# Narrow-head attention values computed once and spread through DRAM, with other settings for the kernel's planner

## The chip, the core and the metric

The kernel runs on one core of a Trainium2 chip. A core has a matrix engine (TensorE, PE in the profile, with its weight loads as PEld), a vector engine (VectorE, DVE), a scalar engine (ScalarE, ACT), a general engine (GpSimd, POOL) and a queue engine (SyncE, SP) that here only issues DMA transfers. Each engine works through its own list of instructions in order and waits on semaphores for the others. Data lie in DRAM (HBM), in the on-chip SBUF and in eight banks of PSUM, where PE writes.

The metric is the device time of one execution in microseconds (us). Three executions and one profiled execution are shown for the kernel before.

## What is computed

Sixteen sequences of 128 tokens by 128 features (`x`) pass through four layers; each layer adds a gated cross-attention to a context of 16 x 77 x 96 (`ctx_768`), and then a gated feed-forward part. All is in fp32.

```python
x = x + tanh(g_xattn[0]) * narrow_attention(layernorm(x), ctx_768)   # 16 heads of 8
x = x + tanh(g_ffn[0])   * top2_of_8_experts(layernorm(x))           # 128 -> 512 -> 128, gelu
x = x + tanh(g_xattn[1]) * wide_attention(layernorm(x), ctx_768)     # 16 heads of 64
x = x + tanh(g_ffn[1])   * weighted_linear_experts(layernorm(x))
x = x + tanh(g_xattn[2]) * one_head_attention(layernorm(x), ctx_768)
x = x + tanh(g_ffn[2])   * top1_of_8_experts(layernorm(x))           # silu
x = x + tanh(g_xattn[3]) * narrow_attention(layernorm(x), ctx_768)   # as in layer 0
x = x + tanh(g_ffn[3])   * ternary_ffn(layernorm(x))
```

The narrow attention, which the change touches:

```python
q = (x @ wq + bq).reshape(B, Sq, 16, 8)
k = (y @ wk + bk).reshape(B, Sk, 16, 8)
v = (y @ wv + bv).reshape(B, Sk, 16, 8)
attn = softmax(einsum('bqhd,bkhd->bhqk', q, k) / sqrt(8))
out = einsum('bhqk,bkhd->bqhd', attn, v).reshape(B, Sq, 128) @ wo + bo
```

## The kernel before

**Groups.** The batch of 16 is worked on in four groups (NG = 4) of four sequences (GB = 4). In names such as `a0_2` or `f2_1`, a is attention and f is feed-forward, the first number the layer, the second the group (for `f0` and `f2`, whose experts take two groups together, the half of the batch).

**Narrow heads** (`narrow_heads`, from L828). The sixteen heads are handled four at a time: the keys of four heads lie side by side, masked so that each head meets only its own eight features, which gives 4 x 77 = 308 key positions (PK). With three chunks of 103 (CH) the attention weights are turned and multiplied with the values. So for each sequence the values must be had in a layout in which the 77 context rows stand four times one after the other, as three chunks of 103 rows by 128 features (309 rows, one of them a pad). `narrow_values` (from L806) makes it by brute force: the host has laid the context four times along its columns (`ctx4`); for each sequence SP loads the 309 columns, PE multiplies them with the value weights in three matmuls of 103 rows, ACT or DVE copies the 103 x 384 result from PSUM (`evac`, L622, which may go to either engine), and POOL multiplies it with the head mask `mine`. A matmul in fp32 is two instructions in the profile, so these are 192 instructions for 32 sequences (layers 0 and 3, 16 each).

**Experts.** In layers 0 and 2, `route_half` ranks the tokens of one half, `send` computes the place of each token by a matmul (`place_ps`), and POOL scatters the rows to DRAM (`sorted_x`) by indirect DMA. `sorted_experts` (L1382) loads the sorted rows (`rows_..`), turns them on PE (`rT_ps`), loads each expert's weights (`wx_..`, 578 KB each) and computes hidden layer (`h_ps`) and output (`y_ps`); outputs go to DRAM (`sorted_y`) through SP and are fetched back by indirect DMA (`take_back`). All these transfers but the indirect ones stand in SP's queue.

**Wide heads.** Layer 1 multiplies the value and output weights of each head into one matrix first (`fused`, L925: `heads1`, `heads2`), sends the values that follow to DRAM (`all_u`, by `send_values`) and loads them back in another layout, in pieces of 256 KB and 52 KB.

**The planner.** The program is first recorded as operations with their dependencies (class `Program`), and only then ordered. Every recorded call is emitted from one place, so nearly all profile lines are L535; a normalisation shows as L710 when it went to ACT and L712 when it went to DVE, and weight loads whose expert is read at run time show as L1411 and L1412. `forward` (L305) is a list scheduler: again and again it places the ready operation that is estimated to start first, with a bias against operations late in the order of the pass (`bias`) and a weight on VectorE's duration (`busy`). SBUF is 680 pages of 64 floats for each partition and PSUM eight banks; a tile takes neighbouring pages from its first to its last user, and the operation that takes pages must wait for the former users. Three settings say who may take them: `reserve` (L353, set at L605) is how many pages must stay free when an operation takes new ones while older tiles have none yet; `ahead` is how far past the oldest operation not yet placed an operation may be and still take new pages; `lead` is how long before its latest useful time a DMA may be placed. `arrange` (L456) runs six rounds of a forward and a backward pass, each giving the order of the next, and keeps the best; `emit` writes the operations out. On the chip nothing of the estimates remains but the order on each engine, the choice between engines and the places of the tiles.

Of the kernel before, what the change touches and what calls it, by code (L numbers as in the profile page):

```python
# [11 lines left out]
F32 = mybir.dt.float32  # L12
# [7 lines left out]
B, S, D = 16, 128, 128  # L20
SK, DC = 77, 96
KP = 112
GB = 4
# [4 lines left out]
PK = 4 * SK  # L28
CH = 103
# [186 lines left out]
class Program:  # L216
# [88 lines left out]
    def forward(self, order, ahead, bias, busy, lead):  # L305
# [21 lines left out]
        ready = set()  # L327
# [35 lines left out]
        while len(out) < len(ops):  # L363
            best = None
            for keep in (True, False):
                for n in ready:
                    op = ops[n]
                    got = None
                    for e, when, us in zip(op.engines, op.when, op.us):
                        t = max(free[e], when)  # L370
                        if e == "tensor" and op.first_mode != mode:
                            t = max(t, free[e] + self.TURN)
                        if e in op.port:
                            t = max(t, port)
                        if op.size:
                            t = max(t, op.latest - lead)
                        if op.table not in (None, table):
                            t += self.LOAD
                        cost = us * weigh[e] + bias * (op.pos - oldest)
                        if best is not None and (t + cost if keep else op.pos) > best[0][0]:  # L380
                            continue
                        if got is None:
                            got = place(op, keep, t)
                        if got is None:
                            break
                        if op.pos > oldest + ahead and got[1] and keep:
                            if not any(x.left == 1 and x.slot >= 0 for x in op.tiles):
                                break
                        t = max(t, got[0])
                        key = (t + cost, op.pos) if keep else (op.pos, t)  # L390
                        if best is None or key < best[0]:
                            best = (key, op, e, t, got[1], us)
                if best is not None:
                    break
            if best is None:
                return None
            _, op, e, t, got, us = best
            op.engine, op.start = e, t
            op.end = clock.run(t, us, op.dense) if e == "tensor" else t + us
            free[e] = op.end  # L400
            if e in op.port:
                port = op.end
            if op.table is not None:
                table = op.table
            if e == "tensor":
                mode = op.mode
            if op.after:
                wire = max(wire, op.end) + op.size / self.RATE
                op.end = wire + op.after
            for tl, i in got:  # L410
                tl.slot = i
                spaces[tl.room].take(i, tl.pages)
                unplaced[tl.room].remove(tl.nth)
            ready.discard(op.n)
            out.append(op.n)
            for m in self.back[op.n]:
                ops[m].left -= 1
                if not ops[m].left:
                    get_ready(ops[m])
            for tl in op.tiles:  # L420
                tl.left -= 1
                if not tl.left:
                    when = max(u.end + self.LAG[u.engine] for u in tl.users)
                    spaces[tl.room].give(tl.slot, tl.pages, when)
            while oldest < len(ops) and ops[order[oldest]].end is not None:
                oldest += 1
# [26 lines left out]
            op.latest = length - ends[n]  # L453
        return sorted(range(len(ops)), key=lambda n: (-ends[n], n))

    def arrange(self, rounds=6, ahead=400, bias=0.002, busy=0.3, lead=10.0):  # L456

        ops = self.ops
        self.back = [[] for _ in ops]
        for op in ops:  # L460
            for d in op.deps:
                self.back[d].append(op.n)
        order, best = sorted(range(len(ops)), key=lambda n: ops[n].order), None
        for _ in range(rounds):
            length = self.forward(order, ahead, bias, busy, lead)
            if length is None:
                break
            if best is None or length < best[0]:
                places = {t: t.slot for op in ops for t in op.tiles}
                best = length, [(op.start, op.end, op.engine) for op in ops], places  # L470
            order = self.backward()
        assert best is not None, "no room for any tile"
        self.length, times, places = best
        for op, (op.start, op.end, op.engine) in zip(ops, times):
            pass
        for t, t.slot in places.items():
            pass
        return sorted(ops, key=lambda op: (op.start, op.n))
# [107 lines left out]

@with_exitstack
def tile_gated_blocks(
    ctx: ExitStack, tc: tile.TileContext, x, ctxa, ctx4, cols, rows, b2s, emb, wqo0, wkv0, wx0,
    wq1, wk1, wv1, wo1, we1, wq2, wkv2, wx2, wqo3, wkv3, wf3, out,  # L590
):
    whole = ctx.enter_context(tc.tile_pool(name="whole", bufs=1))
    psum = ctx.enter_context(tc.tile_pool(name="psum", bufs=1, space=PSUM))

    slots = {
        "mv": 4, "st": 6, "ve": 4, "rstd": 4, "mx": 6, "rs1": 5, "rs2": 4, "off": 4,
    }
    low = "middle at v3 ys back junk wT g_gt8 g_eq8 g_lt8"
    shared = {
        "sc": ("psum", True), "bank": ("psum", False),  # L600
        **{tag: ("sbuf", False) for tag in low.split()},
        **{tag: ("sbuf", True) for tag in ("large", "kk", "heads1", "heads2", "we1_sb")},
    }
    pages = {"sbuf": 680, "psum": 8}
    nc = Program(tc.nc, tc, slots, pages, shared, {"sbuf": 20, "psum": 2})  # L605

    class Tiles:
        def tile(self, shape, dtype=F32, tag=None, name=None):
# [2 lines left out]
    sb = Tiles()  # L611
# [7 lines left out]
    def mm_tile(name):  # L619
        return sb.tile([P, 512], F32, tag="bank", name=name)  # L620

    def evac(o, i):  # L622
        nc.either.copy_any(o, i)
# [17 lines left out]
    def col(name, i=0, n=None):  # L641
        at, w = COLS[name]
        return cs[:, at + i : at + (w if n is None else i + n)]
# [16 lines left out]
    for i, layer in enumerate((0, 1, 3)):  # L660
        o = bos[:, i * D : (i + 1) * D]
# [141 lines left out]

    def narrow_values(g, wv, n):  # L806
        got = []
        for b in range(GB):
            at = (g * GB + b) * PK
            cx = sb.tile([KP, 3 * CH], F32, tag="v3", name=f"cx_{n}_{b}")  # L810
            nc.sync.dma_start(cx, ctx4[:, at : at + 3 * CH])
            vp = mm_tile(f"v_ps_{n}_{b}")[:, : 3 * D]
            with nc.together():
                for c in range(3):
                    nc.tensor.matmul(
                        vp[:CH, c * D : (c + 1) * D],
                        lhsT=cx[: DC + 1, c * CH : (c + 1) * CH], rhs=wv,
                        start=True, stop=True,
                    )
            vr = sb.tile([CH, 3, 4, 32], F32, tag="v3", name=f"vr_{n}_{b}")  # L820
            evac(vr, vp[:CH].rearrange("p (c k d) -> p c k d", c=3, k=4))
            vb = sb.tile([CH, 3, 4, 32], F32, tag="v3", name=f"vb_{n}_{b}")
            mask = mine[:CH].rearrange("p c h d -> p c (h d)")[:, :, None, :].to_broadcast([CH, 3, 4, 32])
            nc.gpsimd.tensor_tensor(vb, vr, mask, ALU.mult)
            got.append(vb)
        return got

    def narrow_heads(layer, wqo, wkv, bq, row, t, groups):  # L828
        for g in groups:
            n = f"a{layer}_{g}"  # L830
# [10 lines left out]
                col("hmask")[:, None, :, None].to_broadcast(shape),  # L841
                ALU.mult,
            )
            vbs = narrow_values(g, wkv[: DC + 1, D : 2 * D], n)
            xnT = transposed(layernorm(g, n), n)
            add_row(g, row)
            q = q_proj(xnT, wqo[:, :D], bq, n)
# [759 lines left out]
    def gate(i):  # L1607
        return tg[:, i : i + 1]
# [3 lines left out]
    for t in sorted_x:  # L1612
        k = t.shape[0] // P
        nc.gpsimd.dma_start(
            t.rearrange("(k p) d -> p k d", p=P), zero[:, None, :].to_broadcast([P, k, D])
        )
    a0 = (0, wqo0_sb, wkv0_sb, col("bq0"), 0, gate(0))
    narrow_heads(*a0, [0])

# [62 lines left out]
def _arrays(i):  # L1682
# [3 lines left out]
    def padded(a):  # L1686
        return np.concatenate([a, np.zeros((KP - DC - 1, a.shape[1]), np.float32)], axis=0)
# [6 lines left out]
    def by_head(w):  # L1694
# [25 lines left out]
    }  # L1720
    ctxT = i["ctx_768"].reshape(B * SK, DC).T
    ctxa = np.concatenate([ctxT, np.ones((1, B * SK), np.float32)], axis=0)
    ctx4 = np.broadcast_to(ctxa.reshape(DC + 1, B, 1, SK), (DC + 1, B, 4, SK)).reshape(DC + 1, -1)
    return {
        "x": i["x"],
        "ctxa": padded(ctxa),
        "ctx4": padded(np.concatenate([ctx4, ctx4[:, : 3 * CH - PK]], axis=1)),
        "cols": np.concatenate([parts[n] for n, _ in _WIDTHS], axis=1),
        "rows": _wide(np.concatenate([i["L0_xattn_bo"], i["L1_xattn_bo"], i["L3_xattn_bo"]])),
        "b2s": i["L1_ffn_expert_b"],  # L1730
# [40 lines left out]
```

## Time and profile before

Three executions took 760.32, 767.32 and 770.58 us.

| | us |
|---|---|
| median of three executions | 767.32 |
| the profiled execution, whole | 769.02 |
| its span in the trace | 767.2 |
| mean granted clock of TensorE | 0.911 of full speed |

The profile is that of one execution. Its busy times are of each engine alone; they overlap, and an engine that is busy need not be what the end waits for. The order of the program shows in the stages, whose busy times in us are:

| stage of the trace, us | what is mainly worked on | length | PE | DVE | ACT | POOL | clock |
|---|---|---|---|---|---|---|---|
| 0-115 | narrow heads of layer 0, first half's routing | 115 | 93.35 | 92.33 | 60.25 | 49.68 | 0.93 |
| 115-153 | end of those heads, fused weights | 38 | 31.19 | 13.18 | 13.65 | 11.76 | 0.76 |
| 153-268 | layer 0's experts, layer 1's values | 115 | 97.40 | 41.47 | 57.46 | 30.72 | 0.90 |
| 268-450 | layers 1 and 2 for three groups | 182 | 173.73 | 146.68 | 106.39 | 91.12 | 0.99 |
| 450-479 | last wide heads, loads for layer 2's experts | 29 | 20.90 | 20.01 | 12.33 | 12.43 | 0.92 |
| 479-529 | layer 2's experts, first half | 50 | 49.98 | 27.19 | 31.48 | 11.04 | 0.98 |
| 529-575 | last one-head attention, second half's routing | 46 | 28.10 | 36.73 | 16.02 | 26.63 | 0.65 |
| 575-640 | second half's experts, start of layer 3 | 65 | 60.20 | 38.16 | 40.28 | 13.13 | 0.93 |
| 640-767 | layer 3 | 127.2 | 105.39 | 86.44 | 74.36 | 28.15 | 0.89 |

The clock is what the chip granted to TensorE in that stage. Where the profile names "another core or an unknown queue", the release could not be traced to one of the engines.

### The profile page before, as it was taken

What the parts mean: (1) busy time and instruction counts of PE and PEld (TensorE: products, weight loads), DVE (VectorE), ACT (ScalarE), POOL (GpSimd) and SP (SyncE); (2) the same over time, 40 slices, a digit from 0 to 9 for tenths busy, and PEclk for the clock granted to TensorE, in tenths of its full rate; (3) what the DMA queues carried; (4) which work ended last, traced back from release to release, by engine and by line L of the source; (5) the groups of instructions that cost most, each with busy time, mean ns of one, the idle gap of its engine ahead of it and who ended that gap; (6) DMA issues with size and microseconds to landing.
All of it is one profiled execution on the core that took longest, in us unless ns stands there. A gap on an engine that the chain in (4) does not pass through costs nothing.

```text
span 767.2 us, 15064 instructions
## 1 busy us (share of the span) xinstructions
PE 660.2 (86%) x5408; PEld 528.9 (69%) x5408; DVE 502.2 (65%) x1322; ACT 412.2 (54%) x898; POOL 274.7 (36%) x311
## 2 busy tenths in 40 slices
PE   4889886996698999999998996999557999688996
PEld 3578764776697989567657744988334898565785
DVE  5877993374121478588787886547697833687764
ACT  2756632564254678554555553565325576377853
POOL 4630456025203154485353354106735103521010
PEclk9999985998698999999999998999558999979898
DMA  4100911495448885323324149821105422000000
GB/s 127 44 9 19 310 41 62 157 346 191 130 142 258 272 249 161 106 72 111 85 70 130 36 124 329 280 63 51 35 0 166 153 59 67 15 1 2 1 29 29
DMA packets 86394, 86.87 MB, mean 113 GB/s; under 512 B 6144, under 2 KB 75744, under 8 KB 86320
## 3 DMA queue, kind: packets, MB, share of 16 engines
q1 hardware_dynamic: 80368, 75.55, 31.6%
q0 software_dynamic: 3840, 9.31, 3.6%
q10 hardware_dynamic: 2112, 1.05, 0.5%
q8 instruction: 43, 0.70, 0.4%
q14 instruction: 31, 0.25, 0.1%
HBM read 63.61 MB, written 22.28 MB: 112 GB/s over the span
## 4 chain that ended last, share of the span: by engine, by line
PE 66%; DVE 17%; issue 4%; DMA 4%; ACT 4%; another core or an unknown queue 2%; SPq 2%; POOL 1%; POOLq 0%; DVEq 0%; ACTq 0%
PE banks L535 66%; DVE shared L535 4%; ACT shared L535 3%; DVE mx_a L535 2%; DVE shared L712 2%; SPq L535 2%; DVE x L535 1%; DMA shared<-all_u 1%; DMA shared<-sorted_x 1%; DVE rs_a L535 1%; ACT shared L710 1%; DMA x<-in_x 1%; DVE st_f L535 1%; DMA sorted_y<-shared 1%
## 5 line engine op out<-in xcount | busy, mean ns | idle before, releaser
L535 PE MATMUL banks<-shared 128*128 128x128 f32 (+7 forms) x3040 | 368.8, 325 | 37.2 <-issue 15.7
L535 PEld LDWEIGHTS banks<-shared 128*128 128x128 f32 (+4 forms) x3040 | 294.9, 180 | 93.0 <-issue 45.8
L535 ACT COPY shared<-banks 128x512 f32<-128x512 f32 (+10 forms) x261 | 149.7, 600 | 132.3 <-PE banks L535 116.2
L535 PE MATMUL banks<-ident,shared 128*128 128x128 f32 (+3 forms) x829 | 132.8, 305 | 40.2 <-DVE shared L712 11.5
L535 PEld LDWEIGHTS banks<-ident,shared 128*128 128x128 f32 (+3 forms) x829 | 107.6, 165 | 74.2 <-issue 24.3
L535 ACT ACTIVATE shared<-banks,shared 128x128 f32<-128x128 f32 x304 | 85.6, 378 | 65.8 <-PE banks L535 25.6
L535 ACT ACTIVATE shared<-shared 128x616 f32<-128x616 f32 (+1 forms) x100 | 70.2, 707 | 61.4 <-DVE shared L535 50.1
L535 DVE TENSOR_REDUCE mx_a<-banks 128x8 f32<-128x616 f32 (+1 forms) x100 | 77.2, 773 | 14.4 <-PE banks L535 8.8
L535 DVE TENSOR_TENSOR shared<-banks,shared 128x128 f32<-128x128 f32 (+1 forms) x84 | 26.9, 327 | 88.5 <-PE banks L535 42.9
L535 DVE TENSOR_TENSOR shared<-banks,mx_a 128x616 f32<-128x616 f32 (+1 forms) x100 | 78.1, 781 | 6.3 <-remote 2.0
L535 POOL DMA_INDIRECT shared<-sorted_y,idx_f x48 | 46.7, 973 | 70.1 <-DMA shared<-in_wx 36.7
L535 POOL DMA_INDIRECT sorted_x<-shared,idx_f x48 | 47.4, 988 | 48.1 <-DVE r_both_f L535 23.6
L535 DVE COPY shared<-banks 103x512 f32<-103x512 f32 (+8 forms) x47 | 30.6, 655 | 48.5 <-PE banks L535 44.0
L535 POOL TENSOR_TENSOR shared<-shared,mine 103x384 f32<-103x384 f32 x32 | 32.8, 1038 | 79.0 <-ACT shared L535 54.8
L535 POOL TENSOR_TENSOR shared<-shared,rs_a 128x616 f32<-128x616 f32 x32 | 38.6, 1218 | 52.5 <-DVE rs_a L535 34.6
L535 POOL TENSOR_TENSOR rstd_f<-ve_f,nhalf 128x4 f32<-128x4 f32 x16 | 16.4, 1022 | 83.4 <-DVE ve_f L535 69.4
L535 PE MATMUL banks<-shared,ctx_sb 96*128 96x512 f32 (+1 forms) x80 | 37.9, 598 | 1.7 <-DVE shared L535 1.0
L535 POOL TENSOR_TENSOR x<-x,shared 128x128 f32<-128x128 f32 x64 | 28.7, 456 | 25.2 <-ACT shared L535 13.6
L535 PE MATMUL banks<-ctx_sb,shared 96*128 96x308 f32 x128 | 37.2, 426 | 0.0
L535 POOL TENSOR_TENSOR rstd_a<-ve_a,nhalf 128x4 f32<-128x4 f32 x16 | 16.6, 1038 | 48.4 <-DVE ve_a L535 44.3
L535 ACT ACTIVATE shared<-banks,cols_sb 128x128 f32<-128x128 f32 (+1 forms) x44 | 21.1, 520 | 22.1 <-PE banks L535 18.6
L535 PEld LDWEIGHTS banks<-wkv_sb,shared 97*103 97x103 f32 x192 | 25.8, 191 | 7.5 <-DVE shared L535 3.6
(207 smaller groups left out, 711.3 us busy)
## 6 DMA issues: line engine op xcount, KB each, us to landing
shared<-in_wx SPq DMA_DIRECT2D x60, 578.0 KB
shared<-all_u SPq DMA_DIRECT2D x32, 256.0 KB
sorted_y<-shared SPq DMA_DIRECT2D x76, 64.0 KB
shared<-in_ctx SPq DMA_DIRECT2D x32, 135.2 KB
all_u<-shared SPq DMA_DIRECT2D x14, 308.0 KB
shared<-sorted_x SPq DMA_DIRECT2D x6, 512.0 KB
sorted_x<-shared POOLq DMA_DIRECT2D x2, 1472.0 KB
shared<-sorted_x SPq DMA_DIRECT2D x4, 448.0 KB
```

The costliest lines, as they stand in the source:

```text
L535: getattr(engine, f)(*(_real(a) for a in args), **done)
L710: engine.activation(o.made(), i.made(), AF.Identity, bias=k.made(), scale=r.made())
L712: engine.tensor_scalar(o.made(), i.made(), m.made(), r.made(), ALU.subtract, ALU.mult)
```

## The change

Two things are changed together.

First, `send_narrow_values` computes the values of a group once: four matmuls with the 97 x 77 context as weights (the 97th row holds the ones that carry the bias), one 77 x 512 copy from PSUM, and for each sequence a store by SP that writes the 77 x 128 values four times one below the other into a new DRAM tensor `all_v` (154 KB, in pieces of 512 bytes). `narrow_values` then loads the 309 x 128 rows of each sequence back as three chunks of 103 rows, also through SP and 154 KB, and masks them on POOL as before. The pad row of `all_v` is set to zero by a DMA of POOL at the start. The input `ctx4` is dropped. Over the eight groups this is 32 matmuls in place of 96, eight copies in place of 32, and 64 transfers in place of 32.

Second, the planner's settings: `ahead` from 400 to 800, `bias` from 0.002 to 0.0022, `busy` from 0.3 to 0.07, `lead` from 10.0 to 10.8, the reserve from 20 pages and 2 banks to 0 pages and 1 bank, and ready operations are tried in the order of their numbers.

```diff
-                for n in ready:
+                for n in sorted(ready):
...
-    def arrange(self, rounds=6, ahead=400, bias=0.002, busy=0.3, lead=10.0):
+    def arrange(self, rounds=6, ahead=800, bias=0.0022, busy=0.07, lead=10.8):
...
-    nc = Program(tc.nc, tc, slots, pages, shared, {"sbuf": 20, "psum": 2})
+    nc = Program(tc.nc, tc, slots, pages, shared, {"sbuf": 0, "psum": 1})
...
-    def narrow_values(g, wv, n):
+
+    shape_v = [B, 3 * CH, D]
+    all_v = nc.tile(shape_v, F32, "dram", "all_v", real=tc.dram_tile(shape_v, F32, name="all_v"))
+
+    def send_narrow_values(g, wv, n):
+
+        mm = mm_tile(f"v_ps_{n}").rearrange("p (b d) -> p b d", b=GB)
+        with nc.together():
+            for b in range(GB):
+                nc.tensor.matmul(
+                    mm[:SK, b, :], lhsT=ctx_of(g, b), rhs=wv, start=True, stop=True
+                )
+        v = sb.tile([SK, GB, D], F32, tag="middle", name=f"v_{n}")
+        evac(v, mm[:SK])
+        for b in range(GB):
+            nc.sync.dma_start(
+                all_v[g * GB + b : g * GB + b + 1, :PK].rearrange("o (h k) d -> (o k) h d", h=4),
+                v[:, b, None, :].to_broadcast([SK, 4, D]),
+            )
+
+    def narrow_values(g, n):
         got = []
         for b in range(GB):
-            at = (g * GB + b) * PK
-            cx = sb.tile([KP, 3 * CH], F32, tag="v3", name=f"cx_{n}_{b}")
-            nc.sync.dma_start(cx, ctx4[:, at : at + 3 * CH])
-            vp = mm_tile(f"v_ps_{n}_{b}")[:, : 3 * D]
-            with nc.together():
-                for c in range(3):
-                    nc.tensor.matmul(
-                        vp[:CH, c * D : (c + 1) * D],
-                        lhsT=cx[: DC + 1, c * CH : (c + 1) * CH], rhs=wv,
-                        start=True, stop=True,
-                    )
             vr = sb.tile([CH, 3, 4, 32], F32, tag="v3", name=f"vr_{n}_{b}")
-            evac(vr, vp[:CH].rearrange("p (c k d) -> p c k d", c=3, k=4))
+            nc.sync.dma_start(
+                vr.rearrange("p c k d -> p c (k d)"),
+                all_v[g * GB + b : g * GB + b + 1].rearrange("o (c p) d -> (o p) c d", c=3),
+            )
             vb = sb.tile([CH, 3, 4, 32], F32, tag="v3", name=f"vb_{n}_{b}")
...
-            vbs = narrow_values(g, wkv[: DC + 1, D : 2 * D], n)
+            send_narrow_values(g, wkv[: DC + 1, D : 2 * D], n)
+            vbs = narrow_values(g, n)
...
+    nc.gpsimd.dma_start(all_v[:, PK:].rearrange("b r d -> (b r) d"), zero[:B])
```

With other settings and other operations the planner gives another order on every engine, and another placing of the tiles.

More of the change, by code (lines that the diff above doesn't have):

```diff
@@ L588, in tile_gated_blocks @@
 def tile_gated_blocks(
-    ctx: ExitStack, tc: tile.TileContext, x, ctxa, ctx4, cols, rows, b2s, emb, wqo0, wkv0, wx0,
+    ctx: ExitStack, tc: tile.TileContext, x, ctxa, cols, rows, b2s, emb, wqo0, wkv0, wx0,
     wq1, wk1, wv1, wo1, we1, wq2, wkv2, wx2, wqo3, wkv3, wf3, out,
@@ L1722, in _arrays @@
     ctxa = np.concatenate([ctxT, np.ones((1, B * SK), np.float32)], axis=0)
-    ctx4 = np.broadcast_to(ctxa.reshape(DC + 1, B, 1, SK), (DC + 1, B, 4, SK)).reshape(DC + 1, -1)
     return {
@@ L1726, in _arrays @@
         "ctxa": padded(ctxa),
-        "ctx4": padded(np.concatenate([ctx4, ctx4[:, : 3 * CH - PK]], axis=1)),
         "cols": np.concatenate([parts[n] for n, _ in _WIDTHS], axis=1),
```

## The prediction

> **What bounds the kernel now.** I read the page's busy times, slices and chain shares first, then the groups kept apart by shape, then busy time by stage, then the chain of waits in three windows, and last what the SyncE queue (SPq) waited for.
>
> ```profile
> PE 660.2 (86%) x5408; PEld 528.9 (69%) x5408; DVE 502.2 (65%) x1322; ACT 412.2 (54%) x898; POOL 274.7 (36%) x311
> PE   4889886996698999999998996999557999688996
> DVE  5877993374121478588787886547697833687764
> PEclk9999985998698999999999998999558999979898
> ...
> PE 66%; DVE 17%; issue 4%; DMA 4%; ACT 4%; another core or an unknown queue 2%; SPq 2%; POOL 1%; POOLq 0%; DVEq 0%; ACTq 0%
> ```
> TensorE (PE) is the bound in two thirds of the chain, yet not everywhere: in slices 5 and 6 VectorE (DVE) reads 9, and in slices 29 and 30 PE reads 5 at half clock. The stages (columns: window and length; busy us of PE, weight loads, DVE, ACT, POOL; granted clock; DMA share; GB/s):
>
> ```profile
> 76.80:96.00 19.20, 16.51 (x128) 13.56 (x124) 18.40 (x41) 12.75 (x26) 9.12 (x9) 0.91 0.91 310
> 115.00:134.00 19.00, 12.19 (x95) 8.01 (x95) 6.75 (x17) 4.39 (x7) 11.76 (x12) 0.59 0.18 58
> 192.00:211.00 19.00, 12.21 (x68) 12.03 (x69) 2.67 (x10) 4.57 (x16) 5.47 (x6) 0.66 0.44 130
> 268.00:365.00 97.00, 93.58 (x568) 73.20 (x568) 76.89 (x214) 61.32 (x123) 54.63 (x63) 1.00 0.48 139
> 529.00:575.00 46.00, 28.10 (x134) 20.11 (x133) 36.73 (x99) 16.02 (x32) 26.63 (x23) 0.65 0.09 24
> ```
> Layer 0's attention is bound by DVE (first row), layer 1 by PE (fourth); around 115-134, 192-211 and 529-575 nothing is full and PE idles, then runs slowly.
>
> **The change: value matmuls.** The rows it touches, and the nearest for what replaces them:
>
> ```profile
> L535 PE MATMUL banks<-wkv_sb,shared 97*103 97x128 f32 x192 | 28.3, 300 | 2.9 <-DVE shared L535 2.9
> L535 PE MATMUL banks<-wkv_sb,ctx_sb 97*77 97x128 f32 x32 | 4.5, 274 | 0.6 <-DVE shared L535 0.6
> L535 POOL TENSOR_TENSOR shared<-shared,mine 103x384 f32<-103x384 f32 x32 | 32.8, 1038 | 79.0 <-ACT shared L535 54.8 <-DVE shared L535 13.1 <-DMA shared<-in_wx 7.3
> L535 ACT COPY shared<-banks 103x384 f32<-103x384 f32 x30 | 13.9, 483 | 18.3 <-PE banks L535 16.4 <-DVE shared L535 1.3
> L535 ACT COPY shared<-banks 77x512 f32<-77x512 f32 x8 | 4.7, 584 | 6.5 <-PE banks L535 5.2 <-issue 1.3
> ```
> A 300 ns row includes the pipeline's overlap. By start to start in the trace, one batch's three matmuls (six instructions) take 0.66 us at full clock, a 128-column one 0.22. Removed: 32 x 0.66 = 21.1 us. Added: 8 groups x 4 x 0.22 = 7.1 us. Net -14 us of PE; summing every operation's shortest duration in both orders gives 558.6 and 544.7, -13.9. At the mean clock 0.911 that is -15. Half of it (-7.5) lies in layer 0, where DVE is often the limit: I count half, -3.8. Of layer 3's half, group 0's matmuls lie in the 529-575 hole and count nothing: -5.7. Sum **-9.5**; bounds 0 and -15.
>
> Evacuations: 30 x 0.483 on ACT (two on DVE) become 8 of about 0.58, -9.8 us of ACT. ACT is 54% busy and 4% of the chain: nothing. The 32 masks on POOL stay (32.8 us). DVE keeps 1321 of its 1322 instructions: where DVE binds, nothing is gained. A DMA that zeroes the pad rows joins POOL's queue at the start (a DMA issue there takes 1.64 us in the trace); its landing is first needed by the first value load: nothing, at most 2 us.
>
> **The DRAM trip.** SP loses 32 loads of 135.2 KB and gains 32 stores and 32 loads of 154 KB: 32 more issues at 0.31-0.49 us each, about 13 us of a queue that mostly waits (us in total, times, longest):
>
> ```profile
> SPq L535 <- DVE x L535: 110.3, 5, 84.3
> SPq L535 <- DVE shared L535: 78.2, 38, 15.6
> SPq L535 <- ACT shared L535: 59.1, 13, 18.8
> ```
> The pieces of the chain used below (start, length, what):
>
> ```profile
> 9.79 4.50 DVE shared L712 x2
> ...
> 184.35 10.37 another core or an unknown queue
> ...
> 273.63 5.64 DMA shared<-all_u
> ...
> 412.14 4.25 DMA shared<-all_u
> ...
> 467.84 9.41 DMA shared<-sorted_x
> ...
> 530.88 2.19 DMA sorted_y<-shared
> ```
> What matters is order: the old loads depended on nothing, while a new store stands in SP's queue until its evacuation, a new load until its stores have landed, and all behind wait too: expert weights, sorted rows, layer 1's values. On POOL, a mask now waits for a landing where it waited for ACT, and holds what is queued behind it: the 1.02 us power of the next norm and the dispatch's DMAs. A 64 KB store landed in 2.19 us, 256 KB loads in 4.25 and 5.64 us; between them 154 KB comes to 3.2-3.8, so store plus load 7 us. The Trainium skill ("DMA: Bandwidth & Descriptors", section on the anatomy of one DMA) speaks against trips of this kind: a transfer pays some 2.0 us fixed, most of it the receipt of the target memory, and HBM is the heaviest. Its fit (for the gpsimd path) gives 2.0 + 154/436 = 2.35 us, twice 4.7, an estimate below my rows, which show SP queue transfers amid traffic. I take the rows.
>
> In the new order most value loads have over 8 us of PE work between the last thing SP waits for and their first use. The short ones: the load for batch 0 of layer 0's group 2 has 3.8 us, the one for batch 1 of layer 3's group 0 has 2.6, and the sorted rows of the second layer-2 half behind it 4.1. Load 3.5 plus mask 1.04 against 3.8 and 2.6, and rows against 4.1: stalls of 0.7, 1.9 and about 0, each perhaps followed by half clock. I take **+6**; by the skill's 2.35 us it would be +2; bounds 0 and +34 (below).
>
> **The planner.** All engines' orders change. Placing the same trace durations against the new order:
> - Start: the chain has two normalisations on DVE in 4.50 us; the new order gives three of four to ACT, 0.486 each: **-2**.
> - First layer-2 half: the 9.41 us load above had eight weight loads ahead of it and PE idled 6.6 us. Now five are ahead: **-3** (bounds 0, -6.6).
> - 529-575: the last group's one-head attention now comes before six remaining expert groups. From its transpose to the second half's placement lie 14.1 us of full-clock PE work in 43.2 us before, 20.0 us after: 5.9 us more to fill the holes, **-6**. The skill ("TensorE: Matmul & The Clock Gate", Part 1) says that the clock falls to half after some 3.4 us idle and returns after as long busy; the 0.65 above agrees. By it alone filled holes would also free half of the slow busy time, some 9 us more. The same row has DVE at 36.7 of 46 us, so I leave that out of the sum and keep it for the low end.
> - First layer-0 experts: PE idles 9.3 and 3.7 us near 195 and 202, and weights waited on SP until 153 for pages held by the fused weights. In the new order the fused weights are finished before the experts and 18 weight loads can precede. But the chain there reads "another core or an unknown queue" for 10.4 and 6.4 us, which may be the dispatch's own DMAs and stay: **-5** (bounds 0, -14).
> - Tail: after the last expert group 85.6 us of PE work remain instead of 83.2; it ran at 124.6 us for 83.2: **+3**.
> - Reserves of 0 pages and 1 bank let later work take the last page. Mean PE work between an instruction's gate and itself is unchanged (PE 1.58 to 1.59 us, DVE 2.38 to 2.43): nothing; if this cover is gone, it is the slower rival.
>
> Sum: -9.5 + 6 - 2 - 3 - 6 - 5 + 3 = -16.5. On the profiled execution, 769.0 us (span 767.2 and 1.8 around it), 752.5; the median shown, 767.3, is 1.7 lower: **750 us**.
>
> **Rivals.**
> - Hidden: stalls only move. Every stage but layer 1 has slack on PE, the measured loss of the old order (span less full-clock work) is 767 - 559 = 208 us, and a new order can have as much elsewhere. Only -3 to -5 remains: 763. Against: the two stages named are bare of PE work in the trace.
> - Deeper: holes close too. Experts -14, 529-575 -12, first half -6.6, no new stalls: -9.5 - 2 - 14 - 12 - 6.6 + 3 = -41: 726. For: half clock goes with the holes. Against: DVE's 36.7 of 46.
> - Slower: SP becomes the bound. Eight groups each make it stand for about 3.5 us of landing plus the wait for the evacuation. It decides where this exceeds the cover of what is queued behind. Four places have less than 7 us: the three above and a layer-1 value load (6.8). If each stalls as the 9.41 us row did, 6 us, plus 2.5 at half clock, that is +34; with only the matmul gain left (-9.5) and none of the stage gains, 767.3 - 9.5 + 34 = 792. For: the 248 us of waits in SP's three rows above show how often it stands already. Against: the covers are over 8 us elsewhere.
> - That the planner's edit does only what it says, more reach and fewer spare pages, is not so: ordering, weight of DVE and due times change too. What it brings could come from any of these.
>
> **How the numbers follow.** Sum as forecast 0.42 (own range 738-762), deeper 0.22, hidden 0.17, slower 0.19. Faster by over 2% means below 752.0, about what a measurement of this kernel can tell: 0.6 of the first plus the second, 0.47. Slower (above 782.7) 0.19, within 0.34. The range 719-787 leaves out most of the slower case and the edge of the deep one, under 2 in 10.
>
> **What would show it.** Right: matmuls with 97x77 weights x96 of about 13.5 us busy and none with 97x103; PE busy near 640; the slices around 550 with PE at 7 or more; the placement near 550; no chain piece of all_v. Wrong: chain pieces "DMA shared<-all_v" or SPq waits on all_v landings, PE waiting on POOL's masks, new half-clock slices in the experts or after 600.

## The result, and the profile after

| | before | after |
|---|---|---|
| median, us | 764.74 (4 executions) | 854.44 (4 executions) |
| ratio | 1 | 1.117 (95% interval 1.109 to 1.126) |
| profiled execution's span, us | 767.2 | 852.5 |
| mean granted clock of TensorE | 0.911 | 0.861 |

The change made the kernel 12% slower; the forecast was 750 us. From the page of the changed kernel:

```profile
PE 663.0 (78%) x5280; PEld 525.0 (62%) x5280; DVE 487.7 (57%) x1321; ACT 398.6 (47%) x873; POOL 274.2 (32%) x312
...
PE   5555963737976999999999999997568856367997
...
DVE  6453773423540316967888888666953135264786
...
PEclk9577895658996999999999999998578976676999
...
PE 51%; DMA 22%; SPq 8%; DVE 6%; issue 4%; POOL 4%; ACT 2%; another core or an unknown queue 1%; POOLq 0%; ACTq 0%; DVEq 0%
```

No engine has noticeably more to do than before: PE has 128 instructions fewer, though at the lower clock they take 663.0 us where they took 660.2. In the chain, DMA has gone from 4% to 22% and SP's queue from 2% to 8%. The slices say where: the first thirteen and the last thirteen, with layer 0 and layer 3, which hold the narrow heads; in between PE still reads 9. Of the groups that the prediction named, PE's and ACT's are as forecast (192 instructions gone, 96 with 97 x 77 weights that take 14.1 us), and POOL's masks, themselves unchanged, now have 225.4 us of idle time before them where they had 79.0:

```profile
L535 PE MATMUL banks<-wkv_sb,ctx_sb 97*77 97x128 f32 x96 | 14.1, 288 | 0.2 <-DVE shared L535 0.2
L535 POOL TENSOR_TENSOR shared<-shared,mine 103x384 f32<-103x384 f32 x32 | 32.2, 1005 | 225.4 <-DMA shared<-all_v 208.8 <-ACT shared L535 7.1 <-issue 5.4
```

The chain of the changed kernel between 8 and 90 us, its pieces on `all_v` and on SP (start, length, what):

```profile
12.75 2.86 DMA all_v<-shared
...
15.63 5.77 SPq L535
...
21.49 7.00 SPq L535
...
28.55 11.05 DMA all_v<-shared
...
39.61 8.97 DMA shared<-all_v
...
50.08 16.44 DMA shared<-all_v
...
67.89 15.45 DMA shared<-all_v
```

The first stores land in 2.86 us, less than the forecast had. A load takes 8.97 us, with no other load beside it (only stores), where 3.2 to 3.8 were counted, and one issued while another is under way takes 16. SP itself stands meanwhile in the issue of the next one: the two pieces "SPq" of 5.77 and 7.00 us, where the forecast had 0.3 to 0.5. In the whole trace 22 of the 64 issues of value loads and stores take over 5 us, 137 us together. The view of the tile `all_v` has this for all its transfers (SP's time in the issue, shortest, median and longest in ns; first and last start):

```profile
L535 SPq DMA_DIRECT2D all_v<-shared x32: 283/598/7295, 12.4 to 757.7; - x32
L535 SPq DMA_DIRECT2D shared<-all_v x32: 217/243/7215, 14.8 to 764.2; - x32
```

The next view bears on the reason. It is the DMA traffic of the changed kernel between 17 and 28 us, when such loads were under way and nothing else:

```profile
GB/s 20 22 22 20 22 22 20 22 22 20 22 22 20 22 22 22 20 22 22 20 22 22 20 22 22 20 22 22 20 22 22 20 22 22 20 22 22 20 22 22
DMA packets 468, 0.24 MB, mean 22 GB/s; under 512 B 1, under 2 KB 468, under 8 KB 468
...
q1 hardware_dynamic: 468, 0.24, 7.2%
...
shared<-all_v SPq DMA_DIRECT2D x2, 154.5 KB
```

It is 22 GB/s throughout, one load or two, in a kernel whose traffic before reached 346 GB/s in a slice. At that rate 154.5 KB need 7.2 us, and some 1.8 us remain for what doesn't grow with the bytes, an estimate. The time of the packets is 7.2% of sixteen DMA engines' time, little more than the 6.25% of one. This looks like one of the sixteen DMA engines carrying the whole load. The loads have 103 rows, and 103 is a prime.

### The profile page after: what moved, and what is told of

The parts are those of the page before. It is cut to its first block, busy times and chain, and to the rows that moved or that the text cites. A ratio compares the mean times of both kernels' runs of the same rounds, so it can differ in the third digit from the quotient of the medians.

```text
span 852.5 us, 14829 instructions
## 1 busy us (share of the span) xinstructions
PE 663.0 (78%) x5280; PEld 525.0 (62%) x5280; DVE 487.7 (57%) x1321; ACT 398.6 (47%) x873; POOL 274.2 (32%) x312
## 4 chain that ended last, share of the span: by engine, by line
PE 51%; DMA 22%; SPq 8%; DVE 6%; issue 4%; POOL 4%; ACT 2%; another core or an unknown queue 1%; POOLq 0%; ACTq 0%; DVEq 0%
PE banks L535 51%; DMA shared<-all_v 10%; SPq L535 8%; DMA all_v<-shared 7%; DMA sorted_y<-shared 2%; ACT shared L535 2%; DVE x L535 2%; DVE shared L535 2%; DMA shared<-sorted_x 1%; POOL shared L535 1%; POOL sorted_x L535 1%; DMA shared<-sorted_y,idx_f 1%; POOL x L535 1%; DVE mx_a L535 1%
## 5 line engine op out<-in xcount | busy, mean ns | idle before, releaser
L535 PE MATMUL banks<-shared 128*128 128x128 f32 (+7 forms) x3040 | 375.4, 335 | 86.2 <-POOL shared L535 30.6
L535 PEld LDWEIGHTS banks<-shared 128*128 128x128 f32 (+5 forms) x3040 | 294.1, 182 | 141.8 <-POOL shared L535 33.2
L535 ACT COPY shared<-banks 103x512 f32<-103x512 f32 (+9 forms) x235 | 139.5, 616 | 226.1 <-PE banks L535 160.1
L535 PE MATMUL banks<-ident,shared 128*128 128x128 f32 (+3 forms) x829 | 138.9, 315 | 59.0 <-DVE shared L535 29.4
L535 PEld LDWEIGHTS banks<-ident,shared 128*128 128x128 f32 (+3 forms) x829 | 114.0, 174 | 94.9 <-DVE shared L535 32.9
L535 POOL TENSOR_TENSOR shared<-shared,mine 103x384 f32<-103x384 f32 x32 | 32.2, 1005 | 225.4 <-DMA shared<-all_v 208.8
L535 DVE COPY shared<-banks 128x512 f32<-128x512 f32 (+8 forms) x49 | 31.5, 649 | 32.0 <-PE banks L535 30.2
L535 PE MATMUL banks<-shared,own 103*32 103x128 f32 (+1 forms) x768 | 32.9, 318 | 10.6 <-ACT shared L535 7.1
L535 PEld LDWEIGHTS banks<-shared,own 103*32 103x32 f32 (+1 forms) x768 | 26.7, 130 | 17.0 <-ACT shared L535 8.2
## 6 DMA issues: line engine op xcount, KB each, us to landing
shared<-all_v SPq DMA_DIRECT2D x32, 154.5 KB
```

Of the source, the lines that this page charges most:

```text
L535: getattr(engine, f)(*(_real(a) for a in args), **done)
```

## The experiments

Two other chips, 4 and 11, ran these. On both the kernel before takes 716 to 727 us, with medians of 722 to 724, not 760 to 771, so ratios to the kernel before on the same chip are compared. Where traces of the experiments are set side by side they are from these two; those of the kernel before, of the settings alone and of 112 rows are from chip 11, those of the changed kernel and of the loads cut in two with its order from chip 4. The changed kernel has the ratio 1.145 there:

> The changed kernel itself on the chip that ran the experiments: ratio to the kernel before 1.10 to 1.14 as at first (1.117). It gives the one-engine loads' price against the split version beside it: 0.943/1.117, so 14 to 17% of the changed kernel's time.

Measured: 826.28 us, ratio 1.145 (1.141 to 1.149), a little beyond the upper end of what was expected. So the slowdown is not the first chip's. The value loads and stores show the same pieces as on the first chip, 11.04, 9.40, 16.44 and 15.69 us in the same places.

**Cutting the load in two.** Three theories stood: the number of rows (A), the trip through DRAM as such (B), the planner's settings (C). The first experiment leaves every engine's order and all places in SBUF as they are in the changed kernel, and only issues each load as two.

```diff
-            nc.sync.dma_start(
-                vr.rearrange("p c k d -> p c (k d)"),
-                all_v[g * GB + b : g * GB + b + 1].rearrange("o (c p) d -> (o p) c d", c=3),
-            )
+            dst = vr.rearrange("p c k d -> p c (k d)")
+            src = all_v[g * GB + b : g * GB + b + 1].rearrange("o (c p) d -> (o p) c d", c=3)
+
+            def call(engine, dst=dst, src=src):
+                for p0, p1 in ((0, 96), (96, 103)):
+                    engine.dma_start(dst[p0:p1].made(), src[p0:p1].made())
...
```

> The changed kernel with its order, engine choice and tile places untouched; only each of the 32 loads of all_v is issued as two DMAs, of 96 rows and of 7 rows, in place of one of 103 rows. Theory A (a transfer of 103 rows is carried by one DMA engine, since 103 divides by nothing): the 96 rows spread over 16 engines, a load takes 2.5 to 4 us in place of 7 to 16, SyncE no longer stands 5 to 7 us over the issue of the next transfer, and the time falls to 745 to 775 us. Theory B (the trip through DRAM with its landings is what costs): loads shorten little where they wait for stores, 820 us or more. Theory C (the new planner settings): 835 to 855 us, unchanged.

Measured: 681.32 us, ratio 0.943 (0.935 to 0.951); this expectation was set against a kernel before of 767 us, on which scale 0.943 is 723: further to A's side than A had it (745 to 775). Once more, beside the changed kernel:

> The changed kernel's order with loads of 96 and 7 rows, beside the changed kernel: 0.943 of the kernel before, as before.

Measured: 677.46 us, ratio 0.939 (0.936 to 0.943). With 64 loads for 32, the same bytes and the same order, the changed kernel sheds 18% of its time (677.46/826.28 = 0.820), more than the 14 to 17% expected, and no issue of a value load or store takes over 1.7 us any more. The waits of POOL in the two, first the changed kernel, then the one with loads of 96 and 7 rows, both on chip 4 (us in total, times, longest):

```profile
POOL shared L535 <- DMA shared<-all_v: 204.4, 27, 20.5
```

```profile
POOL shared L535 <- DMA shared<-all_v: 44.2, 7, 19.4
```

And the slices of the latter, where the narrow heads' stages at both ends are fuller again:

```profile
PE   5889979999999999999999999999568996889996
```

This excludes C as the cause of the slowdown, since the settings' order is untouched, and B, since the trip is still made. It doesn't yet tell the number of rows from the cutting itself.

**Two engines.** The same edit with the cut at 94 = 2 x 47:

```diff
-                for p0, p1 in ((0, 96), (96, 103)):
+                for p0, p1 in ((0, 94), (94, 103)):
```

> As the run with 96 and 7 rows, but cut into 94 and 9 rows: 94 is 2 x 47, so by theory A only two engines carry the larger piece, a load takes about half of the one-engine time, 3.5 to 4.5 us, and the time lies between, 765 to 810 us. If the number of rows didn't matter (theories B and C), it is the same as with 96 and 7 rows.

Measured: 709.56 us, ratio 0.982 (0.974 to 0.991), which is 753 on the scale of 767: between the two, if nearer to the fast one than expected (765 to 810). A load is back in the chain with a length of its own, and where such a load is under way almost alone (572.9 to 573.9 us) the traffic is twice that of the 103 rows, and so is the share of sixteen engines' time:

```profile
565.16 5.02 DMA shared<-all_v
...
571.65 5.03 DMA shared<-all_v
```

```profile
DMA packets 85, 0.04 MB, mean 44 GB/s; under 512 B 0, under 2 KB 85, under 8 KB 85
...
q1 hardware_dynamic: 85, 0.04, 14.3%
```

The two loads have the same number of pieces as with 96 and 7, so cutting isn't what helps. The length follows from two engines: 94 of 103 rows are 141 KB, at 44 GB/s 3.3 us, and with the 1.8 us left over from the one-engine load 5.1 us, an estimate. Measured are 5.02 and 5.03, a little longer than the 3.5 to 4.5 expected, which had halved the whole load and with it those 1.8 us.

**One load of a good size.** Chunks of 112 rows, one DMA:

```diff
-CH = 103
+CH = 112
...
-    nc.gpsimd.dma_start(all_v[:, PK:].rearrange("b r d -> (b r) d"), zero[:B])
+    pad = 3 * CH - PK
+    nc.gpsimd.dma_start(all_v[:, PK:], zero[:B, None, :].to_broadcast([B, pad, D]))
```

> The changed kernel with chunks of 112 rows in place of 103 (three chunks of 112, 112 and 84 used rows), so that each load of all_v is one DMA of 112 rows. The planner sees other sizes and gives an order of its own. Theory A (the number of engines follows from the number of rows): 112 is 7 x 16, loads land in 2.5 to 4 us, ratio to the kernel before 0.93 to 0.96 as with 96 and 7 rows. If it was not the rows but some other effect of cutting the load in two, ratio 1.08 or more.

Measured: 696.81 us, ratio 0.965 (0.960 to 0.969). More bytes and a single DMA, and the slowdown is gone: it was the 103. POOL's masks wait 14.0 us in all for these loads, and the one load that stands in the chain, issued 0.9 us behind another, takes less than a fourth of the 8.97 us:

```profile
609.03 2.11 DMA shared<-all_v
```

But it is 2% slower than the version with 96 and 7 rows and a little outside the range expected. Waits for these loads can hardly be the reason, as that version has more of them; the planner saw other sizes and gave another order. From the first group's turn in layer 1 (`xnT_ps_a1_0`) to the last output of the second group (`y_a1_1_3`) it takes 92.2 us, against 89.0 and 91.1 in the two traces with 96 and 7 rows, and in the stretch with the second routing (from `rT_ps_2_0` to `place_ps_f2_1`) 96.2 against 79.2 in both. So two orders from the same settings, where little else than the size of a chunk differs, can lie 2% apart.

**The parts one by one.** New values with the former settings (the change without its edits to `forward`, `arrange` and the reserve):

> The values through DRAM as in the change (103 rows in one load), with the planner's former settings. Theory A: the loads still take 7 us and more each, 810 to 880 us. Theory B: the same. Theory C: 755 to 775 us.

Measured: 843.3 us, ratio 1.166 (1.156 to 1.176), 894 on the scale of 767, more than any theory had: the slowdown needs no new settings, and C falls again. The kernel before with the new settings alone (no `all_v`), run twice:

> The kernel before with the planner's new settings alone, no all_v. Theories A and B: the slowdown is gone, 750 to 775 us. Theory C: 840 us or more.

> The new settings alone once more, beside the run with 112 rows on the same chip, to tell what the values through DRAM are worth when their loads spread: 0.956 as before. If the removed matmul work counts as in the sum (9.5 us of 767, less some stalls), the run with 112 rows is 0.5 to 1.5% faster than this one; if the trip eats it, the two are equal or this one is faster.

Measured: 690.56 us, ratio 0.956 (0.949 to 0.964), and 692.74 us, ratio 0.959 (0.954 to 0.963). On the scale of 767 that is 734 and 735, a larger gain than expected. And the values in loads of 96 and 7 rows with the former settings:

> The values through DRAM in loads of 96 and 7 rows, with the planner's former settings. If the two parts of the change add up: the ratio of the split with the new settings over that of the settings alone, 0.943/0.956 = 0.986, so 0.98 to 0.99. If the trip needs the new settings' order to be hidden: 1.00 or more.

Measured: 702.3 us, ratio 0.970 (0.965 to 0.975), better than either expectation. With the loads spread, the parts are:

| ratio to before | former settings | new settings |
|---|---|---|
| values as before | 1 | 0.956, 0.959 |
| through DRAM, 103 rows | 1.166 | 1.145 |
| through DRAM, 96 and 7 rows | 0.970 | 0.943, 0.939 |

Both parts are gains, and together bring a little less than their product (0.970 x 0.958 = 0.929, measured 0.941); as each entry has an order of its own, this difference isn't explained here. The version at the lower right beats both kernels: 5.9% under the kernel before and 18% under the change as it was made.

**Which settings.** The forecast had put the reserve at nothing. Its value went alone into the kernel before, and then everything but it:

```diff
-    nc = Program(tc.nc, tc, slots, pages, shared, {"sbuf": 20, "psum": 2})
+    nc = Program(tc.nc, tc, slots, pages, shared, {"sbuf": 0, "psum": 1})
```

> The kernel before with only the reserve changed, to 0 pages and 1 bank. If the gain of the settings comes from letting later work take the last pages: 0.96 to 0.97. If it comes from the other settings (reach, weight of VectorE, bias, due times, sorted trial): 0.99 to 1.01. By the prediction the reserve itself is worth nothing.

Measured: 723.57 us, ratio 1.004 (1.001 to 1.006).

> The kernel before with all the new settings but the reserve, which stays at 20 pages and 2 banks: the complement of the run beside it. 0.96 if the other settings bring the gain, 0.99 to 1.01 if the reserve does, and 0.97 to 0.98 for both if each brings a part.

Measured: 706.32 us, ratio 0.979 (0.974 to 0.983). Alone the reserve is worth nothing; with the other settings, which bring 2.1%, its being small goes with another 2%. As two orders of one setting can lie as far apart, the second half of this isn't shown to be the reserve's doing rather than an accident of the order.

**The kernel before, again.** One execution, for its trace on chip 11:

> The kernel before, unchanged, for a trace from the same chip as the runs beside it: ratio 1.00. Its stages tell whether the gain of the new settings (ratio 0.956 in the run with the old values) lies where it was put, at 185-206 us (layer 0's experts), 529-575 us (second half's routing) and 470-477 us, or elsewhere.

Measured: 720.92 us. The row of busy times between 172 and 211 us, layer 0's experts, where in the first trace PE was busy for 25 of 39 us (columns as in the prediction):

```profile
172.00:211.00 39.00, 39.00 (x309) 36.45 (x308) 10.66 (x35) 23.11 (x74) 16.67 (x18) 1.00 0.72 221
```

It is full, at full clock. The holes of the first trace there, which its chain put down to "another core or an unknown queue" (10.37 and 6.42 us), do not belong to the kernel's order, and they are more than one execution's accident: the changed kernel has them too on the first chip and not on chip 4. The same 399 instructions of these experts, first on the first chip, with the longest such piece of its chain there, then on chip 4:

```profile
233.00:297.00 64.00, 50.80 (x399) 49.11 (x398) 18.82 (x72) 34.56 (x104) 15.50 (x17) 0.87 0.35 112
```

```profile
255.03 7.00 another core or an unknown queue
```

```profile
224.00:270.00 46.00, 46.00 (x399) 45.09 (x398) 18.79 (x72) 33.60 (x104) 15.50 (x17) 1.00 0.66 227
```

From the first of these experts (`h_ps_0_0`) to the last of the first half (`y_ps_0_22`) the old order takes 71.2 us on the first chip and 52.1 on chip 11, the changed one 62.9 and 44.9. So the first chip adds 18 to 19 us here with either order, and none of the twelve pages from the other chips has such a release in its chain. What it is stays open.

## Why the prediction was wrong, point by point

- **The step that failed is the length of a value load.** The prediction read "A 64 KB store landed in 2.19 us, 256 KB loads in 4.25 and 5.64 us; between them 154 KB comes to 3.2-3.8". It interpolated by bytes between transfers of 128 rows, and its lower figure, from the skill's fit, is by bytes as well. The number of rows decided: 9.0 us alone, 16 behind another, 11 for a store behind a load. With it failed the term of "0.31-0.49 us each" for SP's issues: 22 of the 64 took 5.1 to 7.3 us. The kernel before gave the hint, as its inputs of 97 rows, `ctx4` among them, are padded to 112 (KP); the forecast listed those loads and didn't ask why. The Trainium skill has the rule in the page that was cited ("DMA: Bandwidth & Descriptors", section "Why a DMA increments its semaphore by 16 and not by 1"): the number of DMA engines is the largest up to 16 that divides the slowest dimension of both sides, 16 for 128 or 96 partitions, one for 127. The runs agree: 22 GB/s with 103 rows, 44 GB/s with 94, and a load of 2.11 us with 112. By this rule the price could have been worked out beforehand: 154.5 KB over the 27 GiB/s of one engine in the page's specifications is 5.5 us, and with its fixed 2.0 (fitted for the gpsimd path) some 7.5, an estimate, still short of the 9.0 measured but beyond the four short covers that the prediction named (2.6 to 6.8 us).
- **The slower rival was right in its place and wrong in its price and its extent.** It let SP stand for landings and gave 792 us, from four places with short cover. Measured is 854. A load takes 9 to 16 us, not 3.5, and SP stands in the issues besides, so covers of "over 8 us" are too short as well. On chip 4, against the same order with spread loads, the changed kernel loses 81 us up to the first layer-0 expert (35 us with the first two groups and 46 with the next two), nothing from there to the second half's routing, and 71 us after it, in layer 3. The loss runs through both layers with narrow heads, not four places. How much of it comes from the loads' own length and how much from what stands behind them in SP's queue was not separated.
- **The value matmuls, -9.5 us, and the trip's stalls, +6,** net -3.5: with spread loads and the new settings the step from the old values to the new (0.943 and 0.939 against 0.956 and 0.959) is worth 1.4 to 2.0%, 9 to 15 us; with the former ones 3.0%. That is a gain, as forecast, and more than the net of the two terms, though orders differ here and the terms were not timed apart. POOL still waits 44.2 us for `all_v` with spread loads. In the change itself the one-engine loads cost about 150 us (826.28 - 677.46 = 149) where +6 was put.
- **Start, -2:** on the first chip the first scores begin at 17.6 us with the changed kernel against 21.1, -3.5; on the other chips at 17.3 against 19.8, -2.5.
- **First layer-2 half, -3:** PE waited 6.6 us for the sorted rows on the first chip before and 4.4 with the changed kernel, -2.2 (6.8 and 4.6 on the others). With spread loads, or the settings alone, this wait is gone from the list.
- **529-575, -6:** from the transpose of the last group's one-head attention (`xnT_ps_a2_3`) to the placement of the second half (`place_ps_f2_1`), the stretch that the prediction took, 43.2 us became 36.3 on the first chip, -6.9. The rows of busy times, before and after:

```profile
530.40:573.60 43.20, 25.57 (x116) 17.77 (x116) 34.57 (x95) 15.46 (x31) 26.08 (x22) 0.64 0.08 23
```

```profile
570.30:606.60 36.30, 26.03 (x169) 20.38 (x167) 24.30 (x79) 15.15 (x36) 17.65 (x15) 0.80 0.19 54
```

More PE work stands in a shorter stretch, as forecast, and the clock comes back in part, from 0.64 to 0.80, which the sum had left out. Taken from the first sorted rows (`rT_ps_2_0`), with the experts ahead of it, the gain is larger: 94.1 us with the old order on chip 11, 84.4 with the settings alone, 79.2 with both parts and spread loads.
- **Layer 0's experts, -5:** the holes stayed, as the prediction had thought possible. The first chip adds 19 us here with the old order and 18 with the new; the new order is 7 to 8 us shorter between the same two marks on the first chip as on the others, but it has less PE work there. On the other chips there was no hole to close.
- **Tail, +3:** not seen. From the last layer-2 expert to the last output it is 112.8 us with the old order, 113.0 with both parts and spread loads, and 106.7 with the settings alone; part of this is work that the order moved.

The forecast without the rows' mistake, 750 of 767, is 0.978; 0.941 was measured with spread loads. The deeper rival, 726 of 767 (0.947), comes nearest, but in part by luck: 9 of the 24.6 us that it puts beyond the sum lie in the holes of layer 0's experts, which these chips don't have.

## What to carry to other kernels

The length of these DMAs went by how their rows divide among the DMA engines before it went by bytes: give the outer dimension of both sides a multiple of 16, as 96 and 112 are here, or cut off the remainder as a DMA of its own, and be wary of primes. When a transfer in a profile is used as the price of a new one, the number of rows must agree, not only the kilobytes. And two changes made together want to be timed apart: here one gained 4% alone, and the other, for want of a cut at row 96, hid it.

## What the runs showed of the hardware that had not been expected

- Loads of 103 rows moved at 22 GB/s in pieces of 512 bytes and those of 94 rows at 44, as one and two of the sixteen DMA engines would. A load of 103 rows took 9.0 us alone and 16 us behind another; 112 rows, with more bytes, took 2.11.
- While a load of 103 rows was under way, SP stood for 5.1 to 7.3 us in the issue of the next load or store, where most other loads took 0.2 us to issue. Everything behind it in SP's queue waited, and a store issued behind such loads took 11 us, 7.3 of them in its issue, where the first ones took 2.86.
- The kernel before ran in 764.74 us on one chip and in 722 to 724 on two others; the ratio of the changed kernel was 1.117 on the first and 1.145 on chip 4. A hole in a trace can belong to the chip: some 18 us in the same stage in both kernels' traces of the first chip, and in none of the others.
